# Two value products per local block instead of three, and a quarter of the second experts' shared expert issued with the last chunked sequence

## The chip, the cores and the metric

The kernel runs on one core of one Trainium2 chip. The metric is the device time of one execution in microseconds; smaller is better. A comparison takes the median of several runs. The profile is one more execution, recorded by the hardware profiler.

The core has five engines that run side by side, each through its own list of instructions in a fixed order: TensorE (PE: matrix products and transposes, into eight PSUM banks), VectorE (DVE: elementwise work and reductions), ScalarE (ACT: functions such as Exp, Ln and Silu, and copies), GpSimd (POOL) and SyncE (SP, which issues most DMAs). They wait for each other by semaphores. An instruction that waits holds up everything behind it on its engine.

## The reference

The reference is a stack of four layers on `x` (8 sequences of 256 tokens, 128 channels, float32). Every half-layer is `x = layernorm(x + f(x))`, except that the layer sizes differ. The halves are: a gated linear recurrence and a local attention with a feed-forward (run twice); a selective scan (Mamba) and a top-1 mixture of 32 experts; a chunked attention stack and a top-2 mixture of 8 experts with a shared expert; an attention with typed heads and a ternary linear layer. The two parts that the change touches, cut:

```python
# local attention: 8 heads of 64, windows of 64 tokens (w windows of n tokens)
q, k, v = split(h @ wqkv)                       # h: x with half its channels shifted by one token
...
bk, bv = look_around(bk), look_around(bv)       # each window sees itself and the window before
sim = einsum('bhwid,bhwjd->bhwij', bq, bk)
mask = (i < j) | (i > j + WINDOW) | (j == -1)   # WINDOW = 64
attn = softmax(where(mask, -max, sim))
out = einsum('bhwij,bhwjd->bhwid', attn, bv)
...
# second experts
routed = ...                                    # top 2 of 8 experts, capacity 320
shared = (silu(x @ sg) * (x @ su)) @ sd         # sg, su: 128 x 1024, sd: 1024 x 128
return shared + routed
```

## The kernel before

The activations stay in on-chip memory as channels by tokens (128 rows, 2048 columns). Six stages follow each other, each with its own division of the eight PSUM banks (`BANKS`; a letter is a tag, the number how many banks it has):

```python
BANKS = {"local_mamba": dict(Q=2, A=1, B=1, M=2, Y=1), "chunked": dict(K=3, A=2, B=1, M=2), "moe2": dict(A=2, B=2, M=3, S=1), "typed": dict(A=2, B=2, O=1, M=1)}
STAGES = ("rglru", "local_mamba", "moe1", "chunked", "moe2", "typed")
```

Within a stage the sequences are generators that record instructions and yield; several are run interleaved. After everything is recorded, a planner, the class `_Order`, puts the instructions of all engines in order: a list scheduler that knows what depends on what, takes the length of each form of instruction from a table (`LENGTHS`, a pair of how long the engine is held and when the result is there, in ns) or a formula, adds an offset to the priority of each engine, tile and stage (`BIAS`), and charges an instruction that would change TensorE's mode (a product with 32 or 64 columns after one of 128, or the reverse) or ScalarE's function table (`STAY`). What it chooses is then imposed as the order of each engine's list. The function tables come in sets. To the planner, Exp and Ln share one set (it puts the combined set's load at `exp_ln`, L900), Silu has another, Gelu a third; where the order has an Ln or an Exp after another set and no such load ahead of it, each function loads a set of its own. Copies, squares and the like belong to every set.

**The local stage.** A local block handles one sequence of one of the two local layers, 16 blocks in all; the eight Mamba sequences, with their long scans on VectorE (L1306, 64 of them), run beside the later ones. A block shifts its input (`h`), makes queries and keys (`local_qk`: products qk, rotation on VectorE L1090 and L1092, squares L1085, norms rn L1098 and L1099, transposes qkt, copies L1111), then values (`local_attention`): `v` has three slots of 128 tokens by 512, which start at tokens 0, 64 and 128. Each slot is one 128x512 product into a Q bank (vps, recorded as two instructions, since float32 runs in two passes) and one ScalarE copy (L1128). Scores are made for tokens 0 to 127 against keys 0 to 127, for tokens 128 to 191 against keys 64 to 191, and for tokens 192 to 255 against keys 128 to 255 (`parts`); a mask ("band", 128 rows by two times 128 keys) is first written to the score bank by a product with the identity. Softmax (L1148 to L1158), transposes and the products o with `v` follow.

**The chunked stage.** Eight sequences, three at a time, each through two attentions (la, sa, with 32-column score and value products, sc and vps) and two feed-forwards (lf, pf: products hps, Relu fh L1875, products out, norm L1785 to L1791). At the end of a sequence the result is transposed back (out L1983, norm, squares L1988, zt L1797, copy L1989 to `x_chunked`), its router logits are made (lg), its rows are stored to DRAM (`rows_chunked`) by SP, and it is routed: `route2` holds Ln and Exp (four, L1554 and L1555), a running count (cum, a product), another Exp (L1606), and POOL's scatters of rows (L1623). The last sequence (b = 7) also starts the load of the shared expert's weights (`weights_shared`), into tiles that its attentions no longer need.

**The second experts.** The shared expert is done in four quarters of 512 tokens (`shared(i)`), each eight steps: gate and up product (pg and pu, 128x512), Silu on ScalarE (L2052), multiplication on VectorE (L2057), four products into one accumulator (acc). `shared(0)` is issued before and around the last routing and the transposes of the rows that were scattered and read back (bt, L1650, in `rows_of`); then the eight routed experts; then gathers of their results on POOL (L1658, 32 in this stage), one for each step of `shared(1)`, `shared(2)` and `shared(3)`, with the results of sequence 0 and its typed inputs advanced step by step during the last two.

Of the kernel before, what the change touches and what calls it, by code (L numbers as in the profile page):

```python
# [14 lines left out]
F32 = mybir.dt.float32  # L15
# [8 lines left out]
P = 128  # L24
B = 8
S = 256
# [55 lines left out]
def _tables():  # L82
# [65 lines left out]
    madd("band", np.concatenate([mask((i < k0) | (i > k0 + 64)), mask((k0 < w) | (k0 > w + 64))], 1))  # L148
# [163 lines left out]
class _Order:  # L312
# [14 lines left out]
    STAY = dict(PE=80, ACT=740)  # L327
    BIAS = {
        "ACT  1": 100, "ACT  5": 585, "ACT bt 3": 5, "ACT bt 5": -775, "ACT d 2": -425, "ACT da 2": -45, "ACT e 2": -5, "ACT e 4": 965, "ACT e 6": -20,
        "ACT got 3": 575, "ACT h 2": -200, "ACT ix 4": 15, "ACT k 2": 265, "ACT lavp 2": 210, "ACT lnrs 1": -10, "ACT lnrs 2": -160, "ACT lnsq 1": -135,  # L330
        "ACT lnsq 2": 15, "ACT ot 2": 10, "ACT ptsb 2": -595, "ACT ptsb 6": -515, "ACT q 2": 20, "ACT qsq 2": 10, "ACT r 2": -5, "ACT rg 1": 10,
        "ACT rg 2": -915, "ACT rn 2": 15, "ACT rs 4": 340, "ACT rs 6": -690, "ACT s 6": 200, "ACT sakq 2": -10, "ACT sg 3": -550, "ACT sh 5": -2525,
        "ACT spe 1": -220, "ACT spt 1": -50, "ACT st 6": 100, "ACT sz 2": 280, "ACT v 2": 885, "ACT vs 4": 320, "ACT xchunked 2": 15, "ACT xs 2": -610,
        "DVE biasfull 3": -335, "DVE biaspart 3": -20, "DVE bt 5": -5, "DVE c 1": 590, "DVE centre 0": 320, "DVE d 2": 10, "DVE decaypart 4": -600,
        "DVE e 4": 570, "DVE four 4": 100, "DVE fs 4": -70, "DVE gate 4": 340, "DVE get 2": 200, "DVE got 4": 530, "DVE identb 0": -50, "DVE k 6": 500,
        "DVE lg 2": 2240, "DVE lo 4": -265, "DVE mv 4": -660, "DVE mv 5": 100, "DVE mv 6": -485, "DVE nm 2": -3975, "DVE nm 6": 4960, "DVE nth 4": -45,
        "DVE oh 2": -725, "DVE oh 5": -10, "DVE ptsb 2": -3895, "DVE ptsb 6": 895, "DVE put 4": -395, "DVE put 5": 55, "DVE q 5": -825, "DVE q 6": -475,
        "DVE rc 2": -1225, "DVE rc 6": 10, "DVE route 2": -55, "DVE s 5": 10, "DVE sares 2": 70, "DVE sel 2": -1590, "DVE sg 3": -140, "DVE sm 4": 2720,
        "DVE spl 1": -215, "DVE ss 2": 370, "DVE st 4": 85, "DVE st 6": 1645, "DVE sum 4": 170, "DVE t 2": 440, "DVE u 2": 250, "DVE vs 4": 50,
        "DVE we 4": 1425, "DVE xc 2": 460, "DVE xla 4": -15, "DVE xlocal 2": -5, "DVE xmoe 5": -200, "DVE xmoe 6": -580, "DVE xpf 4": -370,  # L340
        "DVE xrglru 2": 120, "DVE xsa 4": 80, "DVE z 4": -1990, "PE a 2": -100, "PE acc 5": 155, "PE b 2": -35, "PE bt 3": 75, "PE bt 5": 50,
        "PE cum 2": -995, "PE cum 4": -25, "PE cum 5": -615, "PE fold 2": 2915, "PE g 2": -4155, "PE gate 2": 785, "PE kps 4": 135, "PE less 2": 295,
        "PE lg 2": 1680, "PE lg 4": 50, "PE ln 2": -10, "PE o 2": 10, "PE o 6": -10, "PE pg 5": 150, "PE ps 4": -15, "PE pt 4": -130, "PE pu 3": 220,
        "PE py 3": -200, "PE py 5": 170, "PE qk 2": 25, "PE qkt 2": -720, "PE raw 2": -8675, "PE rows 2": 400, "PE sc 2": -50, "PE sc 4": 65, "PE sc 6": 5,
        "PE v 5": 290, "PE vps 2": 4075, "PE vps 4": 25, "PE wo 2": 75, "PE wo 6": -85, "PE wout 2": -115, "PE xin 2": 1180, "PE xps 2": -2540, "PE y 2": 20,
        "PE z 2": -450, "PE zt 5": 560, "PE zt 6": 25, "POOL d 2": 130, "POOL e 6": -30, "POOL got 4": -200, "POOL h 2": 370, "POOL k 5": 400,
        "POOL k 6": 850, "POOL km 6": 1240, "POOL mean 0": 1510, "POOL places 5": -200, "POOL q 6": 20, "POOL rest 4": -65, "POOL rg 1": -800,
        "POOL rg 2": -200, "POOL rot 2": -400, "POOL s 6": -750, "POOL t 2": 550, "POOL zero 0": -655, "POOL zeros 1": 385, "SP bc 2": -970, "SP cst 3": 5,
        "SP got 3": 355, "SP got 5": 350, "SP rottable 0": 80, "SP rows 4": 210, "SP rowschunked 4": -105, "SP vec 0": -830, "SP w 0": 15, "SP w 3": 115,
        "SP wattn 2": 585, "SP wffn 2": 705, "SP wlocal 0": 1175, "SP wmoe 4": 520, "SP xs 2": -105, "SP ybuf 5": -200,  # L350
    }
    LENGTHS = {
        "ACT  LoadActFuncSet  ": (1178, 1283), "ACT d Ln 128x512 128x512": (535, 640), "ACT da Exp 128x255 128x255": (398, 503),
        "ACT e Abs 128x256 128x256": (460, 565), "ACT e Exp 128x128 128x128": (420, 525), "ACT e Exp 128x256 128x256": (461, 566),
        "ACT e Exp 128x512 128x512": (527, 632), "ACT four Exp 128x2 128x2": (100, 205), "ACT got DMACopy 128x512 128x512": (454, 3611),
        "ACT h TensorCopy 64x255 64x255": (295, 400), "ACT lnrs Exp 128x256 128x256": (315, 420), "ACT ot TensorCopy 128x512 128x512": (486, 591),
        "ACT qsq Square 128x512 128x512": (494, 599), "ACT r Relu 128x256 128x256": (460, 565), "ACT rg Exp 128x1020 128x1020": (1039, 1144),
        "ACT rg Exp 128x1024 128x1024": (998, 1103), "ACT rg Ln 128x1024 128x1024": (950, 1055), "ACT rn Exp 128x16 128x16": (110, 215),
        "ACT rn Ln 128x16 128x16": (112, 217), "ACT rs Exp 128x2 128x2": (96, 201), "ACT rs Ln 128x2 128x2": (98, 203),
        "ACT sh Silu 128x512 128x512": (492, 597), "ACT v TensorCopy 128x512 128x512": (485, 590), "ACT xc Identity 128x256 128x256": (460, 565),  # L360
        "ACT xc Silu 128x512 128x512": (526, 631), "ACT xchunked TensorCopy 128x256 128x256": (263, 368), "ACT xmoe Identity 128x256 128x256": (404, 509),
        "ACT xs TensorCopy 33x256 33x256": (257, 362), "ACT xsq Square 128x128 128x128": (297, 402), "DVE biaspart TensorCopy 96x256 96x256": (197, 282),
        "DVE decay TensorScalarPtr 128x512 128x512": (508, 593), "DVE decaypart TensorCopy 128x512 128x512": (331, 416),
        "DVE four TensorScalarPtr 128x4 128x4": (76, 160), "DVE ge TensorScalarPtr 128x256 128x256": (380, 465),
        "DVE ge TensorScalarPtr 85x256 85x256": (372, 457), "DVE got TensorScalarPtr 128x128 128x128": (258, 343),
        "DVE h TensorTensor 128x256 128x256": (312, 397), "DVE hs TensorScalarPtr 128x1024 128x1024": (2189, 2274),
        "DVE hs TensorTensor 128x1024 128x1024": (1116, 1201), "DVE mv BNStatsAggregate 128x2 128x6": (82, 167),
# [404 lines left out]
class _Kernel:  # L772
# [1115 lines left out]
    def chunked(self):  # L1888
# [7 lines left out]
        with (  # L1896
# [58 lines left out]
            def one_sequence(b):  # L1955
# [6 lines left out]
                if b == B - 1:  # L1962
                    self.weights_shared()
# [447 lines left out]
```

## Time and profile before

| | us |
|---|---|
| runs | 1626.48, 1629.37, 1628.97 |
| median | 1628.97 |
| profiled execution | 1644.68 |
| span of its records | 1642.9 |
| mean granted TensorE clock | 0.942 of full |

The busy time of each engine in the span:

| engine | busy us | share | instructions |
|---|---|---|---|
| TensorE | 1417.4 | 86% | 10826 |
| VectorE | 1102.3 | 67% | 2182 |
| ScalarE | 968.6 | 59% | 2656 |
| GpSimd | 587.5 | 36% | 535 |

The stages in this execution, by the first and last instructions of their lines: recurrence to about 45 us, local and Mamba to 800, first experts to 850, chunked to 1270, second experts to 1441, typed to the end. They overlap a little at the borders.

How to read it: TensorE's share is high, yet it is an average over stages in which different engines are full. A line of the form `1277.29 2.08 PE L870 MATMUL pg<-x_chunked,w_shared ... [3.58 <-ACT sh L2052]` says that at 1277.29 us TensorE ran, for 2.08 us, products that write pg, and that it had sat idle for 3.58 us until ScalarE's instruction at L2052 released it. All products are recorded by one helper line (L870), so that they are told apart by their tiles. Consecutive products overlap: the distance of their starts, not the duration, is what one costs.

### The profile page before, as it was taken

To read this page: it belongs to the slowest core of one execution; us is meant where nothing else is said; L and a number is where in the kernel's file an instruction comes from. 1 tells how busy PE (TensorE), PEld (TensorE's weight loads), DVE (VectorE), ACT (ScalarE), POOL (GpSimd) and SP (SyncE) were. 2 spreads that over 40 slices of the span, in tenths; PEclk is the share of its full clock that TensorE was granted. 3 is DMA by queue.
4 is the path that set the end of the run, shared out by engine and by line. 5 is a ranking of instruction groups with operands and counts; after the bars stand their busy time and mean duration, and the time that the engine had idled before them with its cause. 6 is when DMAs were issued, how large, how long until landed. Compare 5 with 4: busy or idle time off the path is not lost. (4 is left out here: it accounts for less than half of the span.)

```text
span 1642.9 us, 28581 instructions
## 1 busy us (share of the span) xinstructions
PE 1417.4 (86%) x10826; PEld 909.4 (55%) x10826; DVE 1102.3 (67%) x2182; ACT 968.6 (59%) x2656; POOL 587.5 (36%) x535
## 2 busy tenths in 40 slices
PE   2688998989898887777579999999998899899997
PEld 1354554545554544334366766777675576556664
DVE  5745568898989898698545557554546333279886
ACT  3777888787978869446125545455453222167775
POOL 1334544535462523101431222212212102467774
PEclk7789999989999999779789999999998899999998
DMA  5000012121212223155430000000000130000000
GB/s 199 1 1 1 1 40 65 40 60 45 65 40 65 53 52 91 52 179 189 151 119 1 8 12 11 10 5 8 32 18 24 46 121 26 26 9 8 5 8 11
DMA packets 45113, 77.97 MB, mean 47 GB/s; under 512 B 5580, under 2 KB 21988, under 8 KB 43824
## 3 DMA queue, kind: packets, MB, share of 16 engines
q1 hardware_dynamic: 39648, 70.02, 14.0%
q0 software_dynamic: 3216, 5.07, 1.1%
q8 instruction: 85, 1.39, 0.4%
q10 hardware_dynamic: 2112, 1.05, 0.2%
q14 instruction: 52, 0.43, 0.1%
HBM read 66.87 MB, written 10.76 MB: 47 GB/s over the span
## 5 line engine op out<-in xcount | busy, mean ns | idle before, releaser
L870 PE MATMUL y<-hs,ident 128*128 128x512 f32 x256 | 139.7, 659 | 35.9 <-DVE hs L1307 35.6
L1158 POOL TENSOR_TENSOR e<-e,rc 128x1024 f32<-128x1024 f32 x32 | 78.0, 2437 | 202.7 <-DVE rc L1157 194.3
L1306 DVE TENSOR_TENSOR_SCAN hs<-da,hs 128x1024 f32<-128x1024 f32 x64 | 149.1, 2331 | 0.2
L2259 ACT ACTIVATE e<-sc,nm 128x128 f32<-128x128 f32 (+1 forms) x256 | 105.2, 427 | 46.6 <-DVE nm L2254 40.3
L1153 ACT ACTIVATE e<-sc,nm,rn 128x128 f32<-128x128 f32 x256 | 114.3, 466 | 13.8 <-DVE nm L1148 13.5
L981 PE MATMUL pt<-ident,e 128*128 128x128 f32 x768 | 114.2, 278 | 9.4 <-POOL e L1158 4.9
L1302 ACT ACTIVATE da<-d,na 128x255 f32<-128x255 f32 x256 | 109.3, 504 | 17.5 <-DVE hs L1306 13.7
L1836 POOL TENSOR_TENSOR e<-e,rc 128x512 f32<-128x512 f32 x32 | 34.0, 1064 | 219.8 <-DVE rc L1835 154.2
L981 PEld LDWEIGHTS pt<-ident,e 128*128 128x128 f32 x768 | 88.5, 141 | 42.5 <-issue 16.1
L2262 POOL TENSOR_TENSOR e<-e,rc 128x1024 f32<-128x1024 f32 x48 | 90.8, 1896 | 39.1 <-DVE rc L2261 32.1
L1105 POOL TENSOR_TENSOR t<-t,t 128x512 f32<-128x512 f32 x64 | 83.9, 1316 | 58.0 <-DVE t L1092 51.6
L1811 ACT COPY kp<-kps 128x512 f32<-128x512 f32 x128 | 74.7, 583 | 49.0 <-PE kps L870 46.4
L1658 POOL DMA_INDIRECT got<-ybuf,get x48 | 45.7, 952 | 159.2 <-DMA ybuf<-ys 97.1
L870 PEld LDWEIGHTS y<-hs,ident 128*128 128x128 f32 x256 | 48.5, 205 | 82.5 <-DVE hs L1307 54.2
L1304 DVE TENSOR_TENSOR hs<-u,bc 128x1024 f32<-128x1024 f32 x64 | 84.3, 1328 | 2.9 <-POOL u L1291 2.9
L1307 DVE TENSOR_TENSOR hs<-hs,bc 128x1024 f32<-128x1024 f32 x64 | 80.6, 1260 | 0.0
L1847 ACT COPY vs<-vps 128x512 f32<-128x512 f32 x64 | 37.4, 585 | 67.1 <-PE vps L870 53.6
L983 DVE COPY ptsb<-pt 128x512 f32<-128x512 f32 x104 | 68.8, 675 | 11.6 <-PE pt L981 9.3
L870 PE MATMUL qk<-w_local,h 128*128 128x512 f32 x128 | 69.3, 631 | 7.5 <-DVE t L1092 7.1
L870 PE MATMUL vps<-sa_vp,x_lf 128*32 128x512 f32 x512 | 68.4, 594 | 0.0
L1847 DVE COPY vs<-vps 128x512 f32<-128x512 f32 x64 | 43.3, 682 | 37.2 <-PE vps L870 25.1
L2057 DVE TENSOR_TENSOR sh<-sh,pu 128x512 f32<-128x512 f32 x32 | 22.0, 688 | 67.1 <-PE pu L870 54.0
(380 smaller groups left out, 3782.4 us busy)
## 6 DMA issues: line engine op xcount, KB each, us to landing
bc<-xs SPq DMA_DIRECT2D x128, 256.0 KB
w_moe<-in_e_dram SPq DMA_DIRECT2D x16, 768.0 KB
w_attn<-in_w_dram SPq DMA_DIRECT2D x4, 1024.0 KB
w_local<-in_w_dram SPq DMA_DIRECT2D x2, 1557.0 KB
places<-zeros SPq DMA_DIRECT2D x2, 1280.0 KB
got<-places SPq DMA_DIRECT2D x6, 256.0 KB
ybuf<-ys SPq DMA_DIRECT2D x8, 160.0 KB
x_in<-in_x_dram SPq DMA_DIRECT2D x1, 1024.0 KB
```

The source lines that it names most:

```text
L870: return self.nc.tensor.matmul(out, lhsT, rhs, start=start, stop=stop)
L981: self.last = self.nc.tensor.transpose(pt[:, j * P : (j + 1) * P], src[:, j * P : (j + 1) * P], self.ident)
L1105: nc.gpsimd.tensor_add(t1, t1, t2)
L1153: nc.scalar.activation(e[:, j, g, :], scs[:, j, g, :], AF.Exp, bias=nm[:, j, g : g + 1], scale=rq[:, j, g : g + 1], accum_out=sm[:, j, g : ...
L1158: nc.gpsimd.tensor_tensor(e, e, rc.unsqueeze(3).to_broadcast([P, 2, 4, P]), ALU.mult)
L1302: nc.scalar.activation(da[:, n, c, 1:S], d[:, c, 1:S], AF.Exp, scale=na[:, i : i + 1])
L1304: nc.vector.tensor_tensor(hs, u.unsqueeze(1).to_broadcast(shp), bn, ALU.mult)
L1306: nc.vector.tensor_tensor_scan(line(hs), line(da), line(hs), 0.0, ALU.mult, ALU.add)
L1307: nc.vector.tensor_tensor(hs, hs, cn, ALU.mult)
L1847: i = copy(v[:, c, :, :].rearrange("p a b -> p (a b)"), ps)
L2259: nc.scalar.activation(e[:, i, :], sc[:, i, :], AF.Exp, bias=nm[:, i : i + 1], accum_out=sm[:, i : i + 1])
L2262: nc.gpsimd.tensor_tensor(e, e, rc.unsqueeze(2).to_broadcast([P, n, keys]), ALU.mult)
```

## The change

**Values.** Two products and two ScalarE copies per block, for tokens 0 to 127 and 128 to 255, go to slots 0 and 2. Slot 1, the middle 128 tokens, is put together from halves of the same two banks by VectorE: rows 64 to 127 of the first bank and rows 0 to 63 of the second stay in their rows, so the slot's halves are swapped (tokens 128 to 191 first, then 64 to 127). The scores of tokens 128 to 191 read their keys with the halves swapped too, and the mask's first 64 rows are rolled by 64 columns.

```diff
-        for a in range(3):
+        for t in range(2):
             ps = self.psum("Q", "vps")
-            self.mm(ps, h[:, 64 * a : 64 * a + P], w[:, l, 1024:1536])
-            nc.scalar.copy(v[:, a, :], ps)
+            self.mm(ps, h[:, t * P : (t + 1) * P], w[:, l, 1024:1536])
+            half = slice(64 - 64 * t, P - 64 * t)
+            nc.scalar.copy(v[:, 2 * t, :], ps)
+            nc.vector.tensor_copy(v[half, 1, :], ps[half, :])
...
+                        keys = k[r, g, k0 : k0 + P]
+                        if k0 == 64:
+                            keys = keys.rearrange("p (a b) -> p a b", a=2)[:, ::-1, :]
+                        self.mm(scs[q0 - t * P : q0 - t * P + n, j, g, :], q[r, g, q0 : q0 + n], keys, False, g == 3)
...
+    late = mask((k0 < w) | (k0 > w + 64))
+    late[:64] = np.roll(late[:64], 64, 1)
```

**The shared expert's first quarter.** `shared` becomes a method with the banks as an argument, and quarter 0 is issued by the last chunked sequence: pg and pu in K banks, the accumulator in one of the two M banks, its hidden tiles in a ring of four. The rows of that quarter lie in the tile of the down weights, which grows from 1024 to 1536 columns.

```diff
+                early = iter(())
                 if b == B - 1:
                     self.weights_shared()
+                    self.norm = None
+                    early = self.shared(0, y, self.s0, work, ("K", "M"), tag="e", bufs=4)
...
+                next(early, None)
                 z = yield from self.ffn(x3, w[:, 1, :], "pf", add, work, small)
+                next(early, None)
+                next(early, None)
                 zt = self.by_channel(z)
...
+                next(early, None)
...
                 z = self.normed(out[:, 0:2, :], work, small, "z")
+                next(early, None)
+                next(early, None)
...
                 nc.scalar.copy(y[:, cs], self.by_channel(z))
+                for _ in early:
+                    pass
...
-        down = self.fw.tile([P, 1024], F32, tag="la_vp", name="w_shared")
+        down = self.fw.tile([P, 1536], F32, tag="la_vp", name="w_shared")
+        down, s0 = down[:, 0:1024], down[:, 1024:]
+        self.s0 = s0.rearrange("p (t d) -> p t d", t=4)
...
+    def shared(self, i, x, s, work, banks=("A", "S"), tag="sh", bufs=None):
+        nc = self.nc
+        cs = bass.ts(i, 512)
+        gu, down = self.wsh
+        acc = self.psum(banks[1], "acc")
+        nc.sync.dma_start(s, self.zrows[512 * i : 512 * (i + 1), :].rearrange("(t p) d -> p t d", p=P))
+        for c in range(8):
+            pg, pu = self.psum(banks[0], "pg"), self.psum(banks[0], "pu")
+            self.mm(pg, gu[:, 0, c * P : (c + 1) * P], x[:, cs])
+            self.mm(pu, gu[:, 1, c * P : (c + 1) * P], x[:, cs])
+            h = work.tile([P, 512], F32, tag=tag, name="sh", bufs=bufs)
+            self.silu = nc.scalar.activation(h, pg, AF.Silu)
...
+            self.paced = nc.vector.tensor_mul(h, h, pu)
+            for t in range(4):
+                ts = slice(t * P, (t + 1) * P)
+                self.mm(acc[:, ts], h[:, ts], down[:, c * P : (c + 1) * P], c == 0 and t == 0, c == 7 and t == 3)
+            yield
+        s = s.rearrange("p t d -> p (t d)")
+        nc.vector.tensor_add(s, acc, s)
```

In `moe2` quarter 1 takes the place of quarter 0 around the routing and bt, and the gathers run two to each step of quarters 2 and 3; sequence 0's results begin with quarter 3.

```diff
-            common = shared(0)
+            common = shared(1)
...
-            for _ in shared(1):
-                next(fetch)
             self.x = y
             first = chain(results(0, self.ty), self.typed_before(0))
             for i in (2, 3):
                 for _ in shared(i):
-                    next(first, None)
+                    next(fetch, None)
+                    if i == 3:
+                        next(first, None)
                     next(fetch, None)
```

**The planner's constants.** `STAY` changes, and both tables are replaced as a whole; so the order of instructions changes in every stage.

```diff
-    STAY = dict(PE=80, ACT=740)
+    STAY = dict(PE=130, ACT=250)
     BIAS = {
-        "ACT  1": 100, "ACT  5": 585, "ACT bt 3": 5, "ACT bt 5": -775, "ACT d 2": -425, "ACT da 2": -45, "ACT e 2": -5, "ACT e 4": 965, "ACT e 6": -20,
...
+        "ACT  1": 90, "ACT bt 5": -65, "ACT da 2": -15, "ACT e 6": 1000, "ACT fh 4": 45, "ACT four 5": -70, "ACT ge 2": 885, "ACT got 3": -650,
...
```

## The prediction

> **What bounds the kernel now.** I read the page's busy tenths first, as a map of the stages (a digit is 41 us; PE is TensorE, DVE VectorE, ACT ScalarE).
>
> ```profile
> PE   2688998989898887777579999999998899899997
> DVE  5745568898989898698545557554546333279886
> ACT  3777888787978869446125545455453222167775
> PEclk7789999989999999779789999999998899999998
> ```
>
> No engine holds the whole span. From 40 to 280 us ScalarE and TensorE lead; from 280 to 640 VectorE and TensorE are both near full; from 860 to 1250 (the chunked stage) TensorE alone; then comes a hole, digit 30, in which all three are low. Windows of 40 us show each sort of stretch (length; busy us and count of PE, PE's weight loads, DVE, ACT, POOL; granted clock, DMA share, GB/s):
>
> ```profile
> 280.00:320.00 40.00, 36.32 (x271) 21.96 (x270) 38.58 (x56) 29.80 (x81) 16.73 (x17) 1.00 0.10 27
> 920.00:960.00 40.00, 39.79 (x434) 28.33 (x436) 23.89 (x70) 20.42 (x49) 7.59 (x8) 1.00 0.03 8
> 1240.00:1280.00 40.00, 29.56 (x286) 19.44 (x279) 24.57 (x140) 14.05 (x44) 13.64 (x15) 0.81 0.09 26
> ```
>
> So a microsecond of VectorE counts where 38.58 of 40 are used, one of TensorE where 39.79 are, and in the last window nothing is full and the clock is 0.81: there the waits decide. The timeline of TensorE (start, busy, operation; in brackets the idle before it and its releaser) shows them:
>
> ```profile
> 1267.78 0.70 PE L1797 MATMUL zt<-ident,z 128*128 128x128 f32 x2 [2.06 <-DVE z L1791]
> 1269.89 2.06 PE L870 MATMUL pg<-x_chunked,w_shared 128*128 128x512 f32 x2
> ...
> 1277.29 2.08 PE L870 MATMUL pg<-x_chunked,w_shared 128*128 128x512 f32 x2 [3.58 <-ACT sh L2052]
> ...
> 1284.15 1.12 PE L870 MATMUL pg<-x_chunked,w_shared 128*128 128x512 f32 x2 [1.70 <-ACT sh L2052]
> ...
> 1288.59 1.04 PE L1650 MATMUL bt<-ident,got 128*128 128x128 f32 x8
> ```
>
> From the last sequence's first feed-forward product (1250.93) to the first transpose of gathered rows, bt (1288.59), 37.66 us pass. Idle before instructions sums to 12.05 (0.40+2.75+0.48+0.62+2.06+0.46+3.58+1.70), and products at half clock lose 4.4 (starts 1269.89, 1271.74, 1273.45 are 1.85 and 1.71 apart, against 0.86 from pg at 1290.35 to pu at 1291.21). Work proper: 21.2. From bt to the start of the typed stage (about 1441.3) it is 152.7 us, mostly TensorE.
>
> **Part 1: values by two products.** Per local block (16 of them) one 128x512 product and one ScalarE copy go, and two VectorE copies of 64 rows come. In the lists of instructions products fall from 48 to 32, ScalarE's copies likewise, and 32 VectorE copies are new: the edit does what it says. Prices:
>
> ```profile
> L870 PE MATMUL vps<-w_local,h x96: 590/592/1219, 58.4 to 622.9; 128*128 128x512 f32 x96
> L1128 ACT COPY v<-vps x48: 564/587/647, 64.8 to 625.8; 128x512 f32<-128x512 f32 x48
> ...
> L1847 DVE COPY vs<-vps 128x512 f32<-128x512 f32 x64 | 43.3, 682 | 37.2 <-PE vps L870 25.1 <-PE out L870 11.8
> L2096 DVE COPY ys<-py 64x128 f32<-64x128 f32 x8 | 2.2, 273 | 0.0
> ```
>
> A product is two records; its spacing, 0.86, is what it costs. A VectorE copy of 64 rows by 512 has no row: the 64x128 copy takes 273 ns and 128x128 ones about 285, so half the rows save nothing, and I price it like 128x512: 682 ns, 0.60 from start to start when back to back (L1090 at 47.95, L1092 at 48.55). The nearest cheaper row is 0.42 (128x256). By the starts of the copies, 22 of the 48 (7.3 blocks) lie before 280 and 8.7 blocks after.
> - Before 280: TensorE is busy 200.94 of 240 us, VectorE 152.38, so its copies (7.3x1.2=8.8) fall into 87.6 idle us. Gain 0 to 7.3x0.86=6.3; I take -4, TensorE's busy share being 84%.
> - After: from 280 to 640 VectorE is busy 322.87 of 360, TensorE 313.81. Loss up to 8.7x2x0.60=10.4 if each copy is on the path, gain up to 8.7x0.86=7.5 if TensorE is. I take +2, VectorE being the fuller by 9 us of 360. Cover: VectorE's 37 idle us; without it the whole 10.4. A product's bank is also held until both copies have read it, and the next qk product waits for the bank; that is in the 10.4.
> - The reversed halves of keys: score products read 128 keys in two pieces. The chunked scores, whose operand lies in pieces, take 272 ns, as long as transposes of one piece (272): 0.
>
> **Part 2: the quarter moved ahead.** Eight steps (gate and up product, Silu, multiplication, four down products) are now issued in the last sequence's tail. The lists put 8 pg, 7 pu and 32 acc more ahead of bt: 15x0.86+8x0.89=20.0 us of TensorE (four acc products 0.89: 1289.46 to 1290.35). What follows bt is shorter by as much. If all went into the hole, bt would come at 1250.93+21.2+20.0=1292.1, and the gain is 20.0-3.5=16.5. But ScalarE stands in the way. The order of its list is Silu, norm (Ln, Exp), Silu, router Exp, Silu, norm and so on: 19 table loads where there was one, since Ln and Exp load a set each there.
>
> ```profile
> 1269.02 0.20 ACT L1555 ACTIVATE four<-four 128x2 f32<-128x2 f32 x1
> ...
> 1275.35 1.28 ACT L2052 ACT_TABLE_LOAD   x1
> ...
> 1283.50 0.60 ACT L2052 ACTIVATE sh<-pg 128x512 f32<-128x512 f32 x1 [6.26 <-issue]
> ```
>
> Up to the last sequence's router Exp (L1555, 1269.02 to 1269.22 before) its list now holds 16 loads x1.283=20.5, 7 Silu x0.60, 6 fh x0.46, 13 small ones x0.20, 4 squares x0.45 and 2 copies x0.37: 32.6 us. From 1252.9, less one load in a wait that was there anyway, this ends at 1284.2 without any wait, and about 1286.6 with those I can trace by hand. From there to bt were 19.4 us, 1.6 of them a queue wait on POOL (its 8 scatters L1623, 1.28 each from 1271.38) that is gone by then: bt at 1302.0 to 1304.4, so 13.4 to 15.8 later with 20.0 less behind it: a gain of 6.6 to 4.1. I take -5. Worst: 18 added loads all in the chain, 18x1.283=23.1, less 20.0: +3.1. The added waits: TensorE's acc products wait for Silu and multiplication, and behind them in its order stand the routing products (cum, lg, zt) of sequences 6 and 7; norms wait on ScalarE behind a Silu whose pg isn't ready. SP moves the quarter's 256 KB of rows between stores it does anyway: 0.
>
> The Trainium skill ("ScalarE: Activation LUTs", section "Table sets: the hidden batching unit") says to batch activations by set, and budgets some 2.7 us for a switch; the list does the opposite. The row here says 1.283. By the page's price the 16 loads would add 16x1.4=22 us, and the gain would turn to a loss of some 17.
>
> The same skill ("TensorE: Matmul & The Clock Gate", Part 1) has the clock halved after an idle window near 3.4 us; here products run at 1.85 already after 2.06 idle. By the row both waits, 2.06 and 3.58, must be filled to win the 4.4 back; by the page the second would do, for the 2.55 lost after it.
>
> **Part 3: other orders.** The planner's constants are all replaced.
> - Startup: seven ScalarE loads from 43.95 to 62.31, three in the new list; TensorE waits there 2.12 and 4.29 for L1111 and L1128 behind loads. 0 to -4x1.283=-5.1; I take -3, part being hidden.
> - Rest of the local stage: 5 more loads, 6.4 of ScalarE, which is busy 291 of 360 us: 0 to +6.4, I take +1, as 69 us are free.
> - Chunked: 11 more pairs of changes between 32-column and full products. Eight sc take 0.22 before the next 32-column group (933.76 to 933.98) and 0.38 before a transpose (936.14 to 936.52): 0.16 a change. Fourteen out products last 1.72 before sc (929.43 to 931.15), 1.63 by the 16 from 1253.27 to 1255.13: 0.09 the other way. 11x0.25=2.8 on an engine with nothing free: 0 to +2.8, I take +2.
> - The gathers: ScalarE waits 11.52 at 1402.79 for a cause that the profile doesn't name, and TensorE stands 6.07 with it and then runs 2.6 longer at half clock. This may move or stay: 0 to -8.7, I take -2. The 32 gathers on POOL (about 41 us) stay covered by two quarters, 16 steps x2.61=42; without that cover a few us of them show.
>
> ```profile
> 1402.79 0.60 ACT L2052 ACTIVATE sh<-pg 128x512 f32<-128x512 f32 x1 [11.52 <-remote]
> ```
>
> **Sum.** -4+2-5-3+1+2-2=-9. The profiled execution took 1644.68 (span 1642.9), 15.7 above the runs' median of 1628.97; I carry the difference over: 1629-9=1620.
>
> **The rivals.**
> - More is won: the moved steps fill the hole to 2 us above its floor (-14), the startup gives all (-5, -6), and the stall goes half (-4); local 0, changes +3: -26, 1603. For it: 12 us of idle and a clock of 0.81. Against: ScalarE's 32.6 us.
> - The copies cancel it: VectorE decides from 280 to 640, +10.4 in place of +2, and TensorE's 4 early don't come: -9+8.4+4=+3.4, 1632, on the line between same and slower. It decides when VectorE's idle there falls under some 5% of the time. For: 38.58 of 40. Against: TensorE waits as little.
> - Slower: ScalarE's table loads are on the path, +3.1 in the tail in place of -5, +6.4 in the local stage in place of +1, and the stall stays (+2): -9+8.1+5.4+2=+6.5, 1635.5. Place: L2052, L1791, L1555 between 1250 and 1310; it decides once bt starts later than 1288.6+20.0=1308.6. For: 18 loads added. Against: ScalarE is busy 14.05 of 40 us there.
>
> **Numbers.** Forecast 0.43, more won 0.18, copies cancel 0.17, slower 0.22. Less than 0.2% (3.3 us) can't be told from no change. The forecast's own range, 1612 to 1627, touches that band slightly (0.01); the third case is half same, half slower. Faster 0.60, same 0.10, slower 0.30. The range 1604 to 1638 leaves the ends of the second and last case out.
>
> **What would show it.** VectorE copies to v of 0.60 to 0.68; VectorE's busy share from 280 to 640 (90% before; 93% with the copies) and the last Mamba result (799.4); the count of loads from 1250 to 1310, bt's start (1302 to 1304) and the clock there; typed starting near 1432. Wrong, if bt comes after 1308 or the Mamba results come later than before.

## The result, and the profile after

The changed kernel takes 1645.88 us (median of six runs, 1638.56 to 1652.06); the kernel before, timed beside it, 1629.17 (six runs, 1626.48 to 1630.90). The ratio is 1.0105, with a 95% interval of 1.0083 to 1.0128: the change costs 17 us where a gain of 9 was forecast, and the time lies outside the range. The recorded execution took 1644.87 us (span 1643.1, clock 0.947).

One thing has to be said before the two records are compared. The same kernel took different times on different chips. The kernel before took 1629 us beside the changed kernel and on the chip of experiments 9 to 12, and 1643 and 1644 on two others; each of these chips was used for one set of runs, so that chip and set can't be told apart. Its record of 1644.68 us is like those of the slower chips, while the record of the changed kernel is from a run beside 1629. So the equal spans of the two records say nothing about the change. Later records of both kernels on one chip help to tell what belongs to which (experiments 1, 5 and 6). Ratios are always taken on one chip; they differ a little from the ratio of the medians.

The page's busy tenths of the changed kernel:

```profile
PE   3688987989798887777479999999999799999996
DVE  5756669998989898597545557654545433488886
ACT  4577788797879769356125454555456522277665
PEclk7789999999999999779789999999999999999998
```

Look at the 31st and 32nd digit, 1232 to 1315 us. Before, TensorE had 8 and 8 there, its clock 8 and 8, ScalarE 3 and 2; now TensorE has 9 and 7 at a clock of 9 and 9, and ScalarE 6 and 5. This is the place where the quarter went, and the table loads with it: 19 loads start between 1250 and 1310 us, as forecast, where there was one. The windows that were shown before (length; busy us and count of PE, PE's weight loads, DVE, ACT, POOL; clock, DMA share, GB/s):

```profile
280.00:320.00 40.00, 35.58 (x243) 20.58 (x241) 39.32 (x59) 27.04 (x74) 20.07 (x16) 1.00 0.10 25
920.00:960.00 40.00, 39.87 (x451) 30.02 (x453) 24.24 (x79) 21.30 (x54) 8.34 (x10) 1.00 0.03 8
1240.00:1280.00 40.00, 36.54 (x337) 24.82 (x329) 19.57 (x83) 27.78 (x49) 6.80 (x8) 1.00 0.03 7
```

VectorE went from 38.58 to 39.32 of 40 in the first, and TensorE from 36.32 down to 35.58: what little room VectorE had is used up, and TensorE waits. In the last, TensorE went from 29.56 to 36.54 and the clock from 0.81 to 1.00, as the early quarter was meant to do, and ScalarE's time doubled, from 14.05 to 27.78. So the moved work does fill the hole; it doesn't follow that the end comes earlier. VectorE's share from 280 to 640 us, for which 93% was forecast, is 90.6% (326.08 of 360): the stretch grew with the work, and a share doesn't show that.

The tail on TensorE (start, busy, operation, idle before and its releaser):

```profile
1297.40 1.13 PE L869 MATMUL pg<-x_chunked,w_shared 128*128 128x512 f32 x2 [2.23 <-ACT sh L2054]
1302.89 2.08 PE L869 MATMUL pg<-x_chunked,w_shared 128*128 128x512 f32 x2 [3.50 <-ACT sh L2054]
1307.96 1.08 PE L869 MATMUL pg<-x_chunked,w_shared 128*128 128x512 f32 x2
1308.88 1.04 PE L1654 MATMUL bt<-ident,got 128*128 128x128 f32 x8
```

The first bt starts at 1308.88. The chunked stage began 4.1 us later than in the record before (855.4 and 851.3, ScalarE's first copy of keys), so bt is 16.2 later by the stage's own clock (1308.88-1288.59-4.1). Up to about 1290 us it is ScalarE that holds the chain. Its timeline reads:

```profile
1260.27 1.28 ACT L1791 ACT_TABLE_LOAD   x1
1261.57 0.20 ACT L1791 ACTIVATE rs<-mv 128x2 f32<-128x2 f32 x1
1261.68 0.46 ACT L1879 ACTIVATE fh<-hps,vec 128x256 f32<-128x256 f32 x1
1262.15 1.28 ACT L1792 ACT_TABLE_LOAD   x1
1263.44 0.20 ACT L1792 ACTIVATE rs<-rs 128x2 f32<-128x2 f32 x1
1263.55 0.46 ACT L1879 ACTIVATE fh<-hps,vec 128x256 f32<-128x256 f32 x1
1264.03 1.28 ACT L2054 ACT_TABLE_LOAD   x1
1265.32 0.60 ACT L2054 ACTIVATE sh<-pg 128x512 f32<-128x512 f32 x1
...
1288.22 0.20 ACT L1559 ACTIVATE four<-four 128x2 f32<-128x2 f32 x1
...
1295.23 0.20 ACT L1610 ACTIVATE four<-four 128x2 f32<-128x2 f32 x1 [3.51 <-DVE four L1609]
...
1302.24 0.60 ACT L2054 ACTIVATE sh<-pg 128x512 f32<-128x512 f32 x1 [4.89 <-issue]
```

A norm of two numbers a row (rs: Ln, then Exp) takes two loads of 1.28 for two instructions of 0.20, and the Silu behind it a third. From 1259.35 to 1291.72 no idle time stands in brackets: ScalarE is busy on end. Behind that it waits: 3.51 us for the routing on VectorE, and 4.89 us in which the DMA that reads the scattered rows back (got, L1647, issued by ScalarE at 1301.20) stands in its list ahead of a Silu that TensorE waits for. In the kernel before, a Silu waited 6.26 us behind the same DMA.

### The profile page after: what moved, and what is told of

Read it like the earlier page. It is cut to its first block, busy times and chain, and to the rows that moved or that the text cites. A ratio compares the mean times of both kernels' runs of the same rounds, so it can differ in the third digit from the quotient of the medians.

```text
span 1643.1 us, 28518 instructions
## 1 busy us (share of the span) xinstructions
PE 1416.4 (86%) x10794; PEld 912.0 (56%) x10794; DVE 1117.3 (68%) x2214; ACT 988.0 (60%) x2659; POOL 582.9 (35%) x535
## 5 line engine op out<-in xcount | busy, mean ns | idle before, releaser
L1162 POOL TENSOR_TENSOR e<-e,rc 128x1024 f32<-128x1024 f32 x32 | 74.0, 2313 | 205.2 <-DVE rc L1161 205.0
L2282 POOL TENSOR_TENSOR e<-e,rc 128x1024 f32<-128x1024 f32 x48 | 90.8, 1896 | 43.5 <-DVE rc L2281 33.2
L1308 DVE TENSOR_TENSOR hs<-u,bc 128x1024 f32<-128x1024 f32 x64 | 82.9, 1310 | 1.4 <-POOL u L1295 1.2
L1851 ACT COPY vs<-vps 128x512 f32<-128x512 f32 x64 | 37.5, 587 | 67.6 <-PE vps L869 55.4
L982 DVE COPY ptsb<-pt 128x512 f32<-128x512 f32 x104 | 69.2, 679 | 12.4 <-PE pt L980 8.0
L869 PE MATMUL sc<-msk,identb 128*128 128x512 bf16 (+2 forms) x224 | 51.1, 355 | 25.6 <-ACT e L1157 25.4
L869 PE MATMUL vps<-sa_vp,x_lf 128*32 128x512 f32 x512 | 72.3, 595 | 0.0
L982 ACT COPY ptsb<-pt 128x512 f32<-128x512 f32 x88 | 51.5, 585 | 29.7 <-PE pt L980 22.0
```

The costliest lines, as they stand in the source:

```text
L869: return self.nc.tensor.matmul(out, lhsT, rhs, start=start, stop=stop)
L982: copy(sb.rearrange("p a b -> p (a b)"), pt)
L1308: nc.vector.tensor_tensor(hs, u.unsqueeze(1).to_broadcast(shp), bn, ALU.mult)
L2282: nc.gpsimd.tensor_tensor(e, e, rc.unsqueeze(2).to_broadcast([P, n, keys]), ALU.mult)
```

## The experiments

Experiments 1 to 4, 5 to 8 and 9 to 12 each shared one chip and the runs of the kernel before there: 1643.31 us (median of seven), 1644.06 (seven) and 1629.35 (21). The expectations of experiments 2 to 4 count from 1629, so that it is the ratios that are to be compared with them. In the marks below, "first scan" is the start of the first Mamba scan on VectorE, "last Mamba" the last x_mamba, and "typed" the stretch from the 25th score product with km to the end.

**1. The kernel before, recorded again.** No edit.

> The kernel before, unchanged, profiled once more. Its recorded execution (1644.68 us) was 15.7 us above the median of its timed runs; the changed kernel's was not (1644.87 beside 1645.88), so the two records can't be set against each other. If the 11.52 us wait of ScalarE in the second experts belonged to that execution alone, this record has no wait of that size there and a span near 1628; if it belongs to the kernel, it comes again and the 15.7 us lie elsewhere.

It took 1640.63 us. The wait came again, 11.63 us at 1398.66, and the marks (first scan, last Mamba, first copy of keys, bt, typed) come within 4.3 us of the first record's. The timed runs beside it took 1643 too. So the 15.7 us between the first record and its timed runs don't belong to one disturbed execution; they go with the chip, as far as these runs can tell.

**2. The code before under the new constants.**

```diff
-    STAY = dict(PE=80, ACT=740)
+    STAY = dict(PE=130, ACT=250)
     BIAS = {
...
```

> The code before with the planner's constants of after (three value products, quarter 0 after the chunked stage). If the new orders cost the time (theory: constants): 1638 to 1648. If the early quarter or the VectorE copies cost it: 1626 to 1633.

1669.04 us, ratio 1.0158 (1.0129 to 1.0187): worse than the changed kernel's 1.0105. Neither theory had a number this high (1638 to 1648 is 1.0055 to 1.0117 of 1629). The constants are no improvement in themselves; they go with the new code, and here and in the next run, its mirror image, code planned with constants made for the other one loses 1.6%. So a time of such a mixture can't be read as the price of one part; only stretches whose lists are the same can be. One is: the typed stage has the changed kernel's lists here, and takes 189.0 us (1476.2 to 1665.2) against 180.0 before.

**3. Two value products under the constants of before.**

```diff
-        for a in range(3):
+        for t in range(2):
...
+            nc.vector.tensor_copy(v[half, 1, :], ps[half, :])
```

> The code before with the values part alone, under the constants of before. If VectorE is the bound from 280 to 640 us and the copies cost it (theory: copies): 1634 to 1640. If they hide and TensorE gains: 1620 to 1627. Theory of the constants or of the tail: within 3 us of 1629.

1671.78 us, ratio 1.0157 (1.0124 to 1.0190): again outside of all that was expected (1634 to 1640 is 1.003 to 1.007). The last Mamba result comes at 828.4 against 795.2 in experiment 1 on the same chip (799.4 in the first record), while from the first experts on the lists are those of the kernel before, and the typed stretch takes 180.1. The whole loss is in the local stage. So the values part does not gain of itself; but since the planner made a new order of that stage for it, the run doesn't say what a copy costs; experiment 9 does.

**4. Everything but the early quarter.** The code of experiment 3 under the new constants.

> Everything of the change but the early quarter: two value products and the constants of after. If the early quarter with its table loads costs the time (theory: tail): 1626 to 1632. If copies or constants do: 1640 to 1650; and if the early quarter itself gains the 4 to 7 us that were forecast for it, 1650 or more.

1658.54 us, ratio 1.0091 (1.0063 to 1.0118), where copies or constants were expected to bring it (1640 to 1650 is 1.007 to 1.013 of 1629). Up to 1240 us and in the typed stage its lists are those of the changed kernel. By the ratio the quarter does nothing (1.0105 with it, and 1.0110 in the next run), but the two aren't on equal terms: the 11.6 us wait of experiment 1 isn't in this record, and it is in the changed kernel's in experiment 5. In records without it, the stretch from the chunked stage's first copy of keys to the first score product with km takes 593.0 us here and 578.6 with the quarter, and 590.3 less 11.6, 578.7, in the kernel before (experiment 6). So under these constants the quarter is worth 14 us, against the order of before, with its wait taken off whole, nothing: a list planned for the quarter and left without it is a poor one. This run doesn't give the quarter's price; it is read from experiment 11.

**5. The changed kernel again.** No edit.

> The changed kernel again, beside runs of the kernel before on the same chip. The first three experiments ran where the kernel before takes 1643 us, 14 more than beside the first measurement of the changed kernel. If the changed kernel's 1646 is not moved by what moves the kernel before (theory: the kernel before has waits that come and go), the two are equal there, 1641 to 1648 each. If both move alike, the changed kernel takes 1655 to 1665 and the ratio stays at 1.01.

1666.10 us, ratio 1.0110 (1.0076 to 1.0145). Both kernels take longer here, the one before by 14.9 us and the changed one by 20.2 (medians), a little more than the 1655 to 1665 expected; within its interval the ratio stays.

**6. The kernel before on the same chip.** No edit.

> The kernel before, profiled on the chip of this set, to be laid beside the record of the changed kernel stage by stage. Theory of the orders: typed stage (from the third softmax unit to the end) 180.0 us as in both earlier records, against 188.3 in the changed kernel. If the typed stage took the same here, the 8.3 would be an effect of the chip.

1644.40 us; typed 180.0 (1462.6 to 1642.6), in the changed kernel on that chip 188.4 (1481.7 to 1670.1). The theory of the orders holds; the chip doesn't do it. From the first copy of keys to the first score product with km it takes 590.3 us, and the changed kernel in experiment 5 599.4, with the long wait of the last section in both.

**7. The last stage's offsets of before.** All entries of `BIAS` that end in 6 are exchanged, nothing else.

```diff
-        "ACT e 6": 1000, "ACT s 6": -300,
+        "ACT e 6": -20, "ACT rs 6": -690, "ACT s 6": 200, "ACT ptsb 6": -515,
...
```

> The changed kernel with the planner's offsets of the last stage alone taken from before: every engine's list is that of the changed kernel up to the typed stage and that of the kernel before in it. Theory (the typed stage lost 8.3 us by its new order): 7 to 9 us less than the changed kernel beside it. Rival (the typed stage ends late because something before it ends late): 0 to 2 us less.

1658.91 us, 7.2 less than the changed kernel beside it by the medians of four runs each, whose ranges overlap; ratio 1.0084 (1.0051 to 1.0117), 4.3 us less than 1.0110. The times alone don't decide, the windows do. The windows of the typed stretch of the kernel before, of the changed kernel and of this one, in this order:

```profile
1462.90:1642.90 180.00, 167.14 (x1561) 101.98 (x1560) 146.16 (x361) 121.02 (x546) 118.66 (x76) 0.97 0.02 7
```

```profile
1454.80:1643.10 188.30, 172.80 (x1561) 103.95 (x1560) 147.44 (x361) 121.77 (x546) 119.11 (x76) 0.97 0.02 7
```

```profile
1476.60:1656.80 180.20, 167.36 (x1561) 102.09 (x1560) 146.18 (x361) 120.95 (x546) 118.72 (x76) 0.97 0.02 7
```

The same 1561 instructions of TensorE at the same clock: in the new order they are 5.7 us longer busy and 2.6 us longer idle, 8.3 in all. That is the price of the new list of a stage that the code change doesn't touch. The 5.6 us more of work are in the score products (sc): without idle time, the distances from each start to the next sum to 69.0 us for the 308 of them, 63.4 before. Changes of mode are not the reason: by the records TensorE goes 152 times from one form of product (rows and columns of the array) to another in this stretch, and 164 times before. Which neighbour makes a score product dearer was not followed up.

**8. Fewer table loads.** Four loads of the set that holds Ln and Exp both are put into ScalarE's list ahead of an Ln that follows a Silu; the ten loads that these Ln and Exp would make for themselves go, six loads fewer in all, and nothing else moves.

```diff
+        for i in order["ACT"]:
...
+                if self.groups[i] != table and f == "Ln" and self.stage[i] == 4 and spare:
+                    ring.append(spare.pop(0))
...
+            ring.append(x)
```

> The changed kernel with four loads of the combined set for Ln and Exp put into ScalarE's list in the tail, so that six loads go; all other lists and orders are the same. Theory (the tail's first transpose waits for ScalarE's loads): first bt 6 to 8 us earlier and the whole 5 to 8 us less. Rival (the loads hide behind TensorE's in-order waits): bt moves under 3 us, the whole under 2.

1657.05 us, 9.0 less than the changed kernel by the medians; ratio 1.0077 (1.0048 to 1.0106), 5.4 us less than 1.0110. The first bt in experiment 5, where the first copy of keys was at 859.9, and here, where it was at 850.9:

```profile
1318.12 1.04 PE L1654 MATMUL bt<-ident,got 128*128 128x128 f32 x8
```

```profile
1300.86 1.04 PE L1676 MATMUL bt<-ident,got 128*128 128x128 f32 x8
```

From the copy to bt it takes 449.9 us instead of 458.2. The tail waits for ScalarE's loads, as the prediction had it.

**9. Narrow copies.** The copies keep their place and their waits and move 64 columns; the products of the other heads read slot 0 instead, so the middle slot's values are left out for seven heads of eight.

```diff
-            nc.vector.tensor_copy(v[half, 1, :], ps[half, :])
+            nc.vector.tensor_copy(v[half, 1, 0:64], ps[half, 0:64])
...
-                        self.mm(o[64 * j : 64 * j + 64, g, qs], v[:, a, hd * 64 : (hd + 1) * 64], pt[:, g, qs])
+                        self.mm(o[64 * j : 64 * j + 64, g, qs], v[:, a if hd == 0 or a != 1 else 0, hd * 64 : (hd + 1) * 64], pt[:, g, qs])
```

> The changed kernel with the VectorE copies of the middle slot cut from 512 to 64 columns; it leaves out the middle slot's other heads (their products read slot 0). Every engine's list keeps its order. Theory (VectorE is the bound from the first scan to the last Mamba result, and 20 of the 32 copies, 0.60 us each, lie on it): that stretch 551 to 557 us before falls by 7 to 9, since a copy of 64 columns still costs some 0.15 to 0.25, and the whole falls by 7 to 11. Rival (the new order of the stretch costs it, not the copies): 0 to 3 us.

1636.95 us, ratio 1.0039 (1.0024 to 1.0054), 0.66% or 10.7 us under the changed kernel's ratio, which was measured in another set of runs; the two intervals leave 5 to 17 us. First the copies by tile, in the changed kernel (durations in ns: least, median, most) and here:

```profile
L1128 ACT COPY v<-vps x32: 564/586/637, 60.9 to 629.2; 128x512 f32<-128x512 f32 x32
L1129 DVE COPY v<-vps x32: 669/688/695, 64.2 to 629.8; 64x512 f32<-64x512 f32 x32
```

```profile
L1130 DVE COPY v<-vps x32: 202/222/228, 63.9 to 622.1; 64x64 f32<-64x64 f32 x32
```

Half the rows save nothing, as was forecast from the 64x128 copy: 688 ns. The planner's table has 197 for the time that this copy holds VectorE; so the order was made as if the copies cost a third of what they do. Whether the right length would give a better order was not tried. Then the windows from the first scan to the last Mamba result, of the kernel before, of the changed kernel and of this one:

```profile
252.70:799.40 546.70, 452.10 (x2421) 262.19 (x2420) 474.35 (x566) 397.25 (x1005) 208.92 (x169) 0.94 0.28 84
```

```profile
249.70:804.10 554.40, 449.22 (x2400) 258.45 (x2398) 486.57 (x586) 402.01 (x1006) 208.05 (x170) 0.94 0.28 82
```

```profile
249.20:794.40 545.20, 443.80 (x2400) 254.74 (x2398) 477.58 (x585) 401.11 (x1006) 210.08 (x170) 0.94 0.29 84
```

Take VectorE's busy time from the length: it idles 72.4, 67.8 and 67.6 us. Its idle time hardly changes with its work: 486.57-474.35=12.2 us more work, 20 copies of 0.61, lengthen the stretch by 7.7, and 9.0 us less shorten it by 9.2. That is how an engine that sets the time shows itself, though it is busy only 87 to 88% of the stretch. One record alone would not carry this: with the same lists the stretch takes 541.3 to 546.7 us in five records of the order before and 548.5 to 557.2 in six of the new one. On the chip of this experiment the narrow copies win only 3.3 us against the new order (experiment 10), and against the mean of the six records 8.0. But the means say the same: VectorE idles 69.3 us in the five (66.8 to 72.3) and 67.2 in the six (63.2 to 71.0).

TensorE has the opposite sign: less work than before (449.22 and 452.10) and a longer stretch. Its largest wait there is for VectorE, in the kernel before and in the changed one (us in total, times, longest):

```profile
PE y L870 <- DVE hs L1307: 35.6, 29, 5.0
```

```profile
PE y L869 <- DVE hs L1311: 37.1, 33, 3.4
```

The PSUM bank that a copy holds is no rival: in the whole changed kernel TensorE's products wait for these copies (L1129) once, for 0.5 us, and its weight loads three times, for 1.4. The rival that the new order of the stretch costs the time has the order unchanged here and keeps at most what is left over the five, 545.2 against 543.7.

**10. Both mends in the changed kernel** (7 and 8 together).

> The changed kernel with both mends: the last stage's offsets of before (7.2 us less in its own experiment) and the combined table loads (9.0 less). If the two are separate terms: 14 to 18 us less than the changed kernel, a ratio of 0.998 to 1.003 to the kernel before. If they share a wait: 9 to 12 less.

1627.92 us, ratio 1.0005 (0.9986 to 1.0024): 1.0% or 16 us under the changed kernel's, as much as the typed window (8.1) and the way to bt (8.3) gave one by one. So the two are separate terms, and together they make good what the change cost.

**11. The early quarter alone**, with three value products and, by stage, the old constants and the old table of lengths outside the chunked stage and the second experts.

```diff
+    STAY_OLD, OLD = dict(PE=80, ACT=740), (0, 1, 2, 3, 6)
...
-        return self.LENGTHS.get(self.form(i)) or self.length(i)
+        return (self.LENGTHS_OLD if self.stage[i] in self.OLD else self.LENGTHS).get(self.form(i)) or self.length(i)
```

> Three value products as before, with the constants of before in all stages but the chunked one and the second experts, so that the lists are those of the kernel before up to the chunked stage and in the typed one; the early quarter and the constants of after in between. Theory (the local and typed stages lost 10 and 8 us, the early quarter is about neutral): 1.000 to 1.006 of the kernel before. Rival (the early quarter is what costs): 1.008 or more.

1632.17 us, ratio 1.0014 (1.0003 to 1.0026): the early quarter, with its orders, costs 2.3 us where 5 to be won were forecast (with the mode changes and the wait in the gathers). On the chip of experiments 5 and 6 the same part of the changed kernel costs 9.1 (599.4 against 590.3). The last Mamba result is at 797.8, the typed stretch takes 180.4, as before.

**12. The early quarter with combined loads.**

> The same with the combined table loads in the tail. Theory (ScalarE's loads hold the tail): 6 to 9 us less than without, first bt 6 to 8 us earlier, and so 0.994 to 1.001 of the kernel before: the one form of this change that may beat it. Rival (once the loads go, the wait in the gathers takes what they gave): less than 3 us.

1621.72 us, ratio 0.9953 (0.9939 to 0.9966): faster than both kernels, by 7.6 us than the one before. The first bt on TensorE, in experiment 11 and here (both stages began at 849.9):

```profile
1303.70 1.04 PE L1886 MATMUL bt<-ident,got 128*128 128x128 f32 x8
```

```profile
1293.70 1.04 PE L1908 MATMUL bt<-ident,got 128*128 128x128 f32 x8
```

Ten microseconds for six loads fewer, 1.7 a load where the row says 1.28; in experiment 8 they were worth 1.4. The Trainium skill's budget ("ScalarE: Activation LUTs", section "Table sets: the hidden batching unit") of some 2.7 us for a switch is above both; its rule, to batch by set and to let Ln and Exp share one, is what this experiment carries out.

## Why the prediction was wrong

By stretches, in us against the kernel before. The first two rows are means over records of the same lists: five with the lists of before there (the first record, and experiments 1, 6, 11 and 12), six with those of the changed kernel (its first record, and 4, 5, 7, 8 and 10). The 9.5 of the second row is such a mean; on the chips of experiments 1 to 4, 5 to 8 and 9 to 12 alone it is 9.3, 12.4 and 4.8.

| stretch | forecast | measured | how |
|---|---|---|---|
| start to first scan | -7 | -4.6 | 254.2 to 249.6 |
| first scan to last Mamba | +3 | +9.5 | 543.7 to 553.2 |
| chunked stage and second experts | -5 | +2.3 | experiment 11 |
| typed stage | 0 | +8.3 | windows of experiment 7 |
| sum | -9 | +15.5 | the runs: +16.7 |

Three steps of the prediction failed, by about as much each: the copies on VectorE (6.5 us off), the gain behind the moved quarter (7.3), and the typed stage, which had no term (8.3). Both of its own signs of being wrong were seen: bt came after 1308 (at 1308.88, 4.1 of it since the stage began later), and the last Mamba result later than before (804.1 and 799.4).

- **Startup and early values (-4 and -3).** Right in kind, a size off by a third. ScalarE has three table loads there instead of seven, and the first scan comes forward. What the missing products add to that is not shown: experiment 2, with three products under the new constants, has its first scan at 250.1, and experiment 3, with two under the old ones, at 258.5.
- **VectorE's copies after the first scan (+2, with +1 for five more loads).** The mechanism was named and its full price worked out, 8.7 blocks by two copies by 0.60, 10.4. (By their starts 21 of the 48 copies of before lie ahead of 280 us, not 22, which makes 9 blocks and 10.8.) The step that failed is the choice between the ends: it was taken at +2 since VectorE was the fuller engine only by a little, and "37 idle us" were counted as cover. The idle time of VectorE was no cover; it stayed about as long as it was when 12 us of work were added. Though VectorE was the fuller engine by only 9 us of 360, it set the time: the stretch grew by 9.5, close to the end at 10.4, and the 7.5 us that TensorE was to gain didn't come, since TensorE waited for VectorE. In the prediction's terms the rival "the copies cancel it" happened, together with two more losses; and it happened with VectorE idle for 12 to 13% of the stretch, and 9% from 280 to 640, where the prediction asked for less than some 5%; no run shows that figure.
- **The quarter in the tail (-5).** The chain up to bt was right. ScalarE's last router Exp was forecast for 1284.2 to 1286.6 and came at 1288.22, that is 1284.1 by the clock of the stage before; bt was forecast 13.4 to 15.8 later, with up to 2.8 for mode changes, and came 16.2 later; in experiment 5 against 6 it came 21.0 later. What was too large is the gain behind bt: 20.0 us less of TensorE's work were all counted. From bt to the first product of the typed stage the kernel before takes 153.0 us (experiment 6), or 141.4 without the 11.6 of the wait in the gathers; the changed kernel 125.2 in its record, which has no such wait: 16.3 less. So the two cancel to 0 in these records, to +2.3 in the timed experiment, and not at all on the chip of experiments 5 and 6 (+9.1, with the wait in both). Which of the steps behind bt kept the other 3.7 us was not followed up.
- **The clock in the tail.** The reading that products run at half clock "already after 2.06 idle" was wrong: TensorE's clock was at half before that idle time began at 1265.72. Windows of the kernel before, and of the changed kernel in experiment 5 (length, busy us and count of TensorE, ..., clock, DMA share, GB/s):

```profile
1261.40:1264.80 3.40, 1.34 (x8) 0.97 (x8) 1.73 (x6) 1.83 (x10) 0.98 (x1) 1.00 0.17 44
1265.00:1267.70 2.70, 0.69 (x2) 0.29 (x2) 2.32 (x15) 0.44 (x3) 0.00 (x0) 0.50 0.01 3
```

```profile
1303.00:1306.40 3.40, 1.15 (x4) 0.66 (x4) 1.52 (x8) 2.08 (x3) 2.65 (x3) 1.00 0.03 7
1306.60:1310.70 4.10, 1.26 (x2) 0.00 (x0) 0.00 (x0) 0.60 (x1) 2.50 (x4) 0.50 0.05 11
```

  "TensorE: Matmul & The Clock Gate" (Part 1) of the Trainium skill has the clock halved after an idle window of some 3.4 us. The record of the changed kernel fits that: full clock after 2.23 us of idle (1.13 for two products at 1297.40), half after 3.50 (2.08 at 1302.89). The two pairs above don't: the clock went to half at the end of 3.4 us in which TensorE had been busy for 1.34 and 1.15 us, and no single wait in them was longer than 2.75. So what must be filled can't be read from the length of one wait, neither by the row nor by the page.
- **The wait in the gathers (-2).** Experiment 5 has it with the change, and the changed kernel's first record has not; it goes with the chip in these records (last section), and was wrongly a term of the sum.
- **Mode changes (+2).** From the last Mamba result to the sixth sequence's end the two kernels take the same time on one chip (408.5 in experiment 6 and 408.6 in 5), and in the first two records 408.7 and 405.5. So they cost less than forecast, or are hidden; no run separates them from the rest of that order.
- **The typed stage (no term).** The prediction went through the new orders stage by stage and left out this one without a reason. All constants were replaced, and TensorE was busy for 136.50 of the 137.10 us from the mark to 1600: a reordering of a full engine is a term of its own, with a bound on both sides. It cost 8.3 us, half of the difference.
- **The base.** The difference of 15.7 us between the record and the runs was rightly carried over; most likely it is a difference of chips, and the forecast's absolute time doesn't suffer from it.

## What to carry to other kernels

An engine that is 87 to 90% busy in a stretch can set its time almost completely, as VectorE does here: its idle time was made of waits that didn't shrink when work was added. So don't count idle time of the fullest engine as cover; test it by thinning one operation while the order stays. When a schedule is planned anew, each stage has a price, those that the edit doesn't touch too; compare the lists, and put the old order back stage by stage. And work that is moved into a hole must not bring another function set into a chain of tiny norms: here six loads decided between a loss of 2 us and a gain of 8. A length in the planner's table that is too short by a factor of three, as the copies' was, should be measured and put right before the plan is judged.

## What the runs showed of the hardware

Times of one kernel differed by chip: 1629 us on one, 1643 and 1644 on two others, and 1646 against 1666 for the changed kernel. Part of it is one wait in the gathers, for which the profile names no releaser ("remote"): of the 27.0 us between the two records of the changed kernel (spans of 1643.1 and 1670.1), 15.9 lie between bt and the typed stage, where it stands. ScalarE in the kernel before (experiment 6), in the changed kernel on the same chip (experiment 5), and in the changed kernel's first record:

```profile
1403.19 0.60 ACT L2052 ACTIVATE sh<-pg 128x512 f32<-128x512 f32 x1 [11.61 <-remote]
```

```profile
1422.82 0.60 ACT L2054 ACTIVATE sh<-pg 128x512 f32<-128x512 f32 x1 [13.51 <-remote]
```

```profile
1401.99 0.60 ACT L2054 ACTIVATE sh<-pg 128x512 f32<-128x512 f32 x1 [2.96 <-PE acc L869]
```

In experiment 5 the gate product that this Silu reads had been started by TensorE at 1409.36, 13 us earlier; TensorE then stands idle 9.16 us and restarts at half clock (a product of 2.07 where it was 1.02). In the first record the same instruction, in the same lists, starts without it, and none of the records of experiments 9 to 12 has it (nor experiment 4, whose lists differ there; experiment 2 has one of 6.5). The records of experiments 1, 3 and 5 to 8 have it, 11.4 to 13.5 us. Lists, code and data are the same, so it isn't the program alone; what ScalarE waits for there the records don't tell, and it stays open.

TensorE's granted clock went to half at 1264.90 us in the kernel before and came back at 1281.97, in the changed kernel at 1302.49 and 1305.90, and in experiment 5 at 1306.49 and 1316.73. These stretches of 17.07, 3.41 and 10.24 us are 5, 1 and 3 times 3.41. So in these records the clock was decided at the ends of periods of 3.41 us, not at the end of a wait.
